# Fixing the order of GpSimd and of the transfer queue in a fused MoE, attention and recurrence kernel

## The chip, the core and the metric

The kernel runs on one core of one Trainium2 chip. The metric is the device time of one execution in microseconds (us). It has five instruction queues: PE (TensorE, matmuls; its weight loads are listed as PEld), ACT (ScalarE), DVE (VectorE), POOL (GpSimd) and SP (SyncE, which here does nothing but issue transfers). Each queue runs its own instructions in the order in which they stand in it, and waits at an instruction until what that needs is there.

## The reference, cut to what matters

The input is 2 sequences of 2048 tokens, 256 numbers each, all in float32. There are four parts, each adding to x:

```python
x = x + 0.5 * _L0_ffn_ref(_layernorm(x))   # 6 experts, top 2 of them per token, plus a shared expert
x = x + _L0_attn_ref(_layernorm(x))        # 16 heads of 16, every query sees all 2048 keys
x = x + 0.5 * _L0_ffn_ref(_layernorm(x))
x = x + 0.5 * _L1_ffn_ref(_layernorm(x))   # two steps of a gated recurrence, 6 + 6 + 2 products
x = x + _L1_attn_ref(_layernorm(x))        # causal, rotated queries and keys, clipped relative positions
x = x + 0.5 * _L1_ffn_ref(_layernorm(x))
```

In the second attention the relative position is clipped at 32, so it is the band of 32 keys before each query that gets its own term from `rel_emb`; the rest is one constant per query.

## The kernel before

**Stages.** The kernel is one Python trace, fully unrolled: `run_moe`, `attention0`, `run_moe`, `recurrence`, `attention1`, `recurrence`. x stays in SBUF. Blocks are of 512 tokens (`TB`), eight of them; scores and sums go through eight PSUM banks of 128 x 512.

**Mixture of experts (`moe`, from L166).** The tokens are treated in two halves. Each half is routed (`route`, `sort`), its normalised rows are scattered by GpSimd's indirect transfers into `places` in DRAM in the order of experts (`scatter`, L307), read back in 37 tiles of 128 rows (`experts`, L350: `tile_in`, `up`, `turn`, `down`), written to `results`, and gathered again with a weight (`combine`, L416, gathers at L423). The first half's gathers run beside the second half's tiles; half of the second half's gathers (`rest`) run inside the recurrence that follows.

**`attention0` (L661).** The work is cut in units: two per step, eight steps per group of 4 heads x 512 queries. In one unit PE does four score products for the largest (`largest`, L715, read by DVE at L719), four for the exponentials (`exponential`, L727, read by ACT at L732) and one sum over keys (`weighted`, L739). The sum is copied from PSUM by ACT (L605) and added to the group's running sum by POOL (L610, `gather`). Everything else (projections, layer norms, divisions) is put in lists of jobs by step. Keys and queries are spread to 32-row slots by small transfers on SP (`spread`, L134); rows of padding come from DRAM too (`pad_keys`, L141).

**`attention1` (L904).** The same in units of its own planner: `Ms`, `Me` are a group's first and last step of largest scores, `Es`, `Ee` of exponentials, `Rs` the step of the sum over relative positions. One group's band goes a long way: `by_position` (L1019) makes the products with `relk`, ACT sends them to DRAM (L1026, on ACT's own queue), `band_load` (L1036, SP, 1280 KB) reads them back skewed, DVE adds them to the scores (L1083), POOL subtracts the maximum (L1097), `band_store` (L1105, SP, 1280 KB) writes them out, `positions_load` (L1182, SP) reads them along the diagonal. Queries and keys are rotated (`rotate`, L959 to L976): ACT copies the projection, DVE exchanges neighbours (L969), POOL does two products and a sum (L971 to L975). When each transfer is emitted is a list `sends` of its own, in units.

**What sets the order.** The whole trace is in `tc.manual_schedule(engines=ENGINES)` with

```python
ENGINES = {mybir.EngineType.PE, mybir.EngineType.Activation, mybir.EngineType.DVE}
```

An engine in that set issues its instructions in the order of the trace. POOL and SP are not in it: a scheduler places their instructions by its own model of when each is ready. Inside `moe`, and inside the first `recurrence`, a second region orders POOL; but these are two regions, and where an instruction of one falls among those of the other is the scheduler's.

Of the kernel before, what the change touches and what calls it, by code (L numbers as in the profile page):

```python
# [17 lines left out]
P = 128  # L18
# [24 lines left out]
def macaron_kernel(ctx: ExitStack, tc: tile.TileContext, t: dict, out: bass.AP):  # L43
# [112 lines left out]
    ENGINES = {mybir.EngineType.PE, mybir.EngineType.Activation, mybir.EngineType.DVE}  # L156
# [9 lines left out]
    def moe(w, ws, gate_w, gate_b, rev, tri, iota, z, behind, last, gathered):  # L166
# [3 lines left out]
        with ExitStack() as s:  # L170
# [179 lines left out]
            def experts(h, exi, between):  # L350

                xT, h_, hT, val = {}, {}, {}, {}
                GROUP = 8

                def tile_in(i):
                    if i % GROUP == 0:
                        n = min(GROUP, NST - i)
                        _, vs = nc.values_load_multi_w_load_instructions(
                            exi[0:1, i : i + n], engines=[mybir.EngineType.PE],
                            min_val=0, max_val=(NE - 1) * EW,  # L360
                            skip_runtime_bounds_check_because="a sum of five comparisons times EW",
                        )
                        for k, v_ in enumerate(vs):
                            val[i + k] = v_
                    xs = wk.tile([P, D], F32, name="xs", bufs=4)
                    nc.sync.dma_start(out=xs, in_=places[h][ts(i, P), :])
                    pt = bank()
                    for kc in range(2):
                        nc.tensor.transpose(pt[:, ts(kc, P)], xs[:, ts(kc, P)], ident)
                    xT[i] = wk.tile([P, D], F32, name="xT")  # L370
                    nc.scalar.copy(xT[i], pt[:, 0:D])  # L371

                def up(i):
                    pu = bank()
                    for kc in range(2):
                        nc.tensor.matmul(  # L376
                            pu, lhsT=xT[i][:, ts(kc, P)], rhs=w[:, kc, ds(val[i], 2 * D)],
                            start=kc == 0, stop=kc == 1,
                        )
                    sg = wk.tile([P, D], F32, name="sg")  # L380
                    nc.scalar.activation(sg, pu[:, 0:D], AF.Silu)  # L381
                    h_[i] = wk.tile([P, D], F32, name="h")
                    nc.vector.tensor_tensor(h_[i], sg, pu[:, D:], ALU.mult)  # L383

                def turn(i):
                    ph = bank()
                    for kc in range(2):
                        nc.tensor.transpose(ph[:, ts(kc, P)], h_[i][:, ts(kc, P)], ident)
                    hT[i] = wk.tile([P, D], F32, name="hT")
                    nc.vector.tensor_copy(hT[i], ph[:, 0:D])  # L390

                def down(i):
                    po = bank()
                    for kc in range(2):
                        nc.tensor.matmul(  # L395
                            po[:, 0:D], lhsT=hT[i][:, ts(kc, P)],
                            rhs=w[:, kc, ds(val[i] + 2 * D, D)],
# [5 lines left out]

                tile_in(0)
                for i in range(NST + 2):
                    between(i)
                    if i + 1 < NST:
                        tile_in(i + 1)
                    if i < NST:
                        up(i)  # L410
                    if 0 <= i - 1 < NST:
                        turn(i - 1)
                    if 0 <= i - 2 < NST:
                        down(i - 2)
# [17 lines left out]
            def first_half(i):  # L432
                if 3 <= i < 3 + HC:
                    combine(0, i - 3)
# [5 lines left out]
            with tc.manual_schedule(engines={mybir.EngineType.Pool}):  # L440
                stats(0)
                stats(1)
                norm(0)
                stats(2)
                norm(1)
                shared_part(0, 0)
                shared_part(0, 1)
                stats(3)
                norm(2)
                shared_part(0, 2)  # L450
                norm(3)
                shared_part(0, 3)
                mul(0)
                stats(4)
                route(0)
                up(1)
                e0 = sort(0)
                stats(5)
                down(0)
                scatter(0)  # L460
                mul(1)
                up(2)
                stats(6)
                up(3)
                mul(2)
                norm(4)
                norm(5)
                stats(7)
                scatter(1)
                scatter(2)  # L470
                scatter(3)
                down(1)
                mul(3)
                down(2)
                norm(6)
                norm(7)
                down(3)
                route(1)
                up(4)
                mul(4)  # L480
                e1 = sort(1)
                down(4)
                up(5)
                mul(5)
                for b in range(HB, NTB):
                    scatter(b)
                down(5)
                experts(0, e0, lambda i: None)
                experts(1, e1, first_half)
                up(6)  # L490
                mul(6)
                chunks = iter(range(HC))

                def rest(n):
                    for _ in range(n):
                        c = next(chunks, None)
                        if c is not None:
                            combine(1, c)
                            last(c)

                rest(2)
                up(7)
                mul(7)
                rest(1)
                down(6)
                rest(1)
                down(7)
                rest(4)
                if gathered is None:
                    rest(HC)  # L510
# [12 lines left out]

    class Pieces:
# [3 lines left out]
        def __init__(self, s, name, norm, weights_o, bias, queries):  # L528
            self.keep = pool(s, name + "_keep")
            self.wk = pool(s, name + "_wk", 2)  # L530
            self.norm, self.wo, self.bias = norm, weights_o, bias
            self.mnegs = []
# [8 lines left out]
            self.cn, self.cT, self.o, self.pTs, self.q = ({} for _ in range(5))  # L541

# [26 lines left out]
        def values(self, v, wv, b, qc, half, row):  # L569

            w = HV * VW
            nc.gpsimd.memset(v[:, :, w:], 0.0)
            dst = v[:, :, 0:w].rearrange("p k (h d) -> p k h d", d=VW)
            nc.gpsimd.memset(dst[:, :, :, DH:], 1.0)
# [10 lines left out]
            else:  # L585
# [4 lines left out]
                )  # L590

# [10 lines left out]
        def gather(self, t, pv, parts, q0=0):  # L602
# [7 lines left out]
            nc.gpsimd.tensor_tensor(o, o, part[:, q0:], ALU.add)  # L610
# [39 lines left out]
    class Jobs(dict):  # L650
        def at(self, step, fn, *args):
            self.setdefault(step, []).append((fn, args))

        def run(self, step):
            for fn, args in self.get(step, ()):
                fn(*args)


    def attention0(norm, tail, wq, wk_, wv, wo, bff):
# [7 lines left out]
        with ExitStack() as s:  # L667
# [25 lines left out]

            def vals(b, half, qc):
                if qc == 0:
                    v[b, half] = vpool.tile([P, NKB, HV * VW + DH - 1], F32, name="v", bufs=3)
# [78 lines left out]

            for step, fn, *args in tail:
                at(PER * NG + step, fn, *args)
            for step in range(min(jobs), max(jobs) + 1):
                todo = jobs.get(step, [])
                for n in range(2):  # L780
                    te, tm = (step - 9) // PER, step // PER
# [11 lines left out]
                    if 0 <= unit < NG * NKB:  # L793
                        weighted(unit // NKB, unit % NKB)

# [135 lines left out]
    def attention1(norm, tail, w, relk, relv, kbias, dramp, skew):  # L931
# [4 lines left out]
        with ExitStack() as s:  # L936
# [24 lines left out]
            def rotate(wa, b, qc, g, bias):  # L961
# [9 lines left out]
                e.tensor_tensor(xa, xa, cos[b, qc], ALU.mult)  # L971
                e.tensor_tensor(xb, xb, sin[b, qc], ALU.mult)
                if bias is not None:
# [549 lines left out]
```

## Time and profile before

| | us |
|---|---|
| median of 3 runs (4281.06 to 4286.72) | 4283.15 |
| profiled execution | 4171.17 |
| its span | 4169.4 |
| PE busy in the span | 4036.9 |
| SP waiting at L1036 (`band_load`), 22 waits | 285.4 |
| SP waiting at L134 for POOL L975 (a rotation), 27 waits | 257.3 |
| SP waiting at L1105 (`band_store`) for POOL L1097, 21 waits | 244.4 |
| POOL waiting at L610 for ACT L605, 610 waits | 1401.6 |

The profiled execution was 112 us shorter than the median. PE is busy for most of the span, but busy time says little alone: the granted clock has to be read beside it, and so has the stage. The stages, by what PE does, are: first mixture 0 to 350, first attention 350 to 2100, second mixture 2100 to 2445, first recurrence 2445 to 2622, second attention 2622 to 3950, last recurrence to the end.

### The profile page before, as it was taken

The numbers are of one execution on the slowest core, as the hardware profiler recorded it, in microseconds if no ns is written. First come the engines' busy times: TensorE is split into PE (matmuls) and PEld (weight loads), VectorE is DVE, ScalarE is ACT, GpSimd is POOL, SyncE is SP. The second block draws the span as 40 slices with busy tenths as digits, with TensorE's granted clock in tenths as the row PEclk, the third lists the DMA queues.
The fourth block names the chain that finished last, engine by engine and source line by source line (L and its number), as shares of the span: only waits on it lengthen the run. The fifth ranks groups of instructions, "written<-read, shape, count | busy, mean of one in ns | idle before, by whom it ended". The sixth has DMA issues, their size and how long they took to land.

```text
span 4169.4 us, 78015 instructions
## 1 busy us (share of the span) xinstructions
PE 4036.9 (97%) x28256; PEld 1967.4 (47%) x28256; DVE 2697.1 (65%) x6122; ACT 2498.5 (60%) x5091; POOL 1692.5 (41%) x1606
## 2 busy tenths in 40 slices
PE   8997999999999999999999989899999999999999
PEld 4665533333333333333356645555554455555445
DVE  6242888888877788888752444666577666667533
ACT  2331488888877888888933322355557666556832
POOL 4254133336433333333442430445545654544510
PEclk9998899999999999999999999999999999999999
DMA  7343000000000000000043410445433344452101
GB/s 254 119 125 86 15 4 4 4 4 4 4 14 14 4 4 4 4 4 5 9 171 118 127 60 5 106 98 114 95 86 67 81 95 92 86 106 53 45 22 41
DMA packets 376879, 245.34 MB, mean 59 GB/s; under 512 B 157232, under 2 KB 349104, under 8 KB 376496
## 3 DMA queue, kind: packets, MB, share of 16 engines
q1 hardware_dynamic: 298160, 198.39, 18.6%
q0 software_dynamic: 12288, 33.57, 2.5%
q10 hardware_dynamic: 66048, 8.39, 1.4%
q8 instruction: 226, 3.70, 0.4%
q14 instruction: 157, 1.29, 0.1%
HBM read 118.36 MB, written 105.12 MB: 54 GB/s over the span
## 4 chain that ended last, share of the span: by engine, by line
PE 84%; POOL 5%; DVE 4%; DMA 3%; issue 2%; SPq 2%; ACT 1%; ACTq 0%; POOLq 0%; DVEq 0%
PE s L727 13%; PE s L739 12%; PE s L715 10%; PE s L146 8%; PE s L376 6%; PE s L1173 6%; PE s L1059 6%; PE s L1144 5%; PE s L395 3%; DMA band<-skew 2%; PE s L642 1%; POOL places L311 1%; PE s L1154 1%; PE s L1158 1%; PE s L1137 1%
## 5 line engine op out<-in xcount | busy, mean ns | idle before, releaser
L610 POOL TENSOR_TENSOR part<-part 128x512 f32<-128x512 f32 (+3 forms) x800 | 962.6, 1203 | 1407.2 <-ACT part L605 1401.6
L719 DVE TENSOR_REDUCE mx<-s 128x1 f32<-128x512 f32 x2048 | 1270.1, 683 | 331.2 <-PE s L715 331.2
L732 ACT ACTIVATE pT<-s 128x512 f32<-128x512 f32 x2048 | 1063.4, 618 | 239.2 <-PE s L715 237.9
L715 PE MATMUL s<-kT,q 32*128 32x512 f32 x4096 | 1031.9, 630 | 0.0
L727 PE MATMUL s<-q,kT 32*128 32x512 f32 x4096 | 1013.6, 615 | 0.0
L1165 ACT ACTIVATE pT<-s 128x512 f32<-128x512 f32 (+3 forms) x1280 | 588.8, 542 | 223.8 <-PE s L1144 122.3
L605 ACT COPY part<-s 128x512 f32<-128x512 f32 (+3 forms) x864 | 506.5, 587 | 287.9 <-PE s L1173 149.7
L727 PEld LDWEIGHTS s<-q,kT 32*128 32x128 f32 x4096 | 417.9, 184 | 467.2 <-DVE mx L719 326.9
L1067 DVE TENSOR_REDUCE mx<-s 128x1 f32<-128x512 f32 (+1 forms) x768 | 473.3, 679 | 179.5 <-PE s L1059 171.9
L739 PE MATMUL s<-pT,v 128*32 128x512 f32 x4096 | 549.9, 605 | 0.4
L715 PEld LDWEIGHTS s<-kT,q 32*128 32x128 f32 x4096 | 426.4, 187 | 125.5 <-ACT pT L732 77.8
L1059 PE MATMUL s<-kT,q 32*128 32x512 f32 (+7 forms) x2240 | 329.6, 433 | 3.6 <-ACT part L605 3.6
L1173 PE MATMUL s<-pT,v 128*32 128x512 f32 (+3 forms) x2560 | 307.9, 549 | 13.1 <-DVE mx L1083 12.8
L376 PE MATMUL s<-we,xT 128*128 x592 | 279.0, 594 | 0.6 <-ACT xT L371 0.6
L1083 DVE CUSTOM_DVE_ANT_0 band<-s,band 128x160 f32<-128x160 f32 (+1 forms) x512 | 156.1, 316 | 173.2 <-PE s L1059 98.9
L1059 PE MATMUL s<-b,q 32*128 32x512 f32 (+7 forms) x1280 | 246.6, 527 | 13.1 <-ACT part L605 8.6
L383 DVE TENSOR_TENSOR h<-sg,s 128x256 f32<-128x256 f32 x148 | 62.4, 421 | 296.3 <-ACT sg L381 296.3
L739 PEld LDWEIGHTS s<-pT,v 128*32 128x32 f32 x4096 | 82.4, 108 | 335.7 <-ACT pT L732 297.4
L1144 PE MATMUL s<-q,kT 32*128 32x512 f32 (+3 forms) x1152 | 235.5, 509 | 0.0
L423 POOL DMA_INDIRECT yg<-results,at x128 | 125.1, 977 | 232.3 <-DMA results<-y 83.1
L1144 PE MATMUL s<-q,b 32*128 32x512 f32 (+3 forms) x896 | 213.8, 583 | 0.0
L1097 POOL TENSOR_TENSOR band<-band,mneg 128x640 f32<-128x640 f32 x128 | 161.1, 1261 | 97.2 <-DVE mneg L1093 91.4
(207 smaller groups left out, 5159.7 us busy)
## 6 DMA issues: line engine op xcount, KB each, us to landing
band<-skew SPq DMA_DIRECT2D x32, 1280.0 KB
pd<-band SPq DMA_DIRECT2D x32, 1280.0 KB
xs<-places SPq DMA_DIRECT2D x148, 128.0 KB
results<-y SPq DMA_DIRECT2D x148, 128.0 KB
places<-zero SPq DMA_DIRECT2D x2, 4736.0 KB
we<-in_we SPq DMA_DIRECT2D x12, 768.0 KB
skew<-s ACTq DMA_DIRECT2D x32, 256.0 KB
s<-pd SPq DMA_DIRECT2D x32, 256.0 KB
```

Source lines behind the costliest of these rows:

```text
L376: nc.tensor.matmul(pu, lhsT=xT[i][:, ts(kc, P)], rhs=w[:, kc, ds(val[i], 2 * D)], start=kc == 0, stop=kc == 1,)
L605: nc.scalar.copy(part[:, q0:], pv[:, q0:])
L610: nc.gpsimd.tensor_tensor(o, o, part[:, q0:], ALU.add)
L715: nc.tensor.matmul(ps, lhsT=q[t][rows(j), ts(qb, P)], rhs=kT[b, g][rows(j), ts(kc, TB)], start=True, stop=True,)
L719: nc.vector.tensor_reduce(mx[t][:, qb * J + j, kc : kc + 1], ps, AX.X, ALU.max)
L727: nc.tensor.matmul(st, lhsT=kT[b, g][rows(j), ts(kb, P)], rhs=q[t][rows(j), :], start=True, stop=True,)
L732: nc.scalar.activation(z.pTs[t, kb, j], st, AF.Exp)
L739: nc.tensor.matmul(pv[rows(j), :], lhsT=v[b, g // 2][:, kb, ds(h * VW, 32)], rhs=z.pTs.pop((t, kb, j)), start=True, stop=True,)
L1059: nc.tensor.matmul(ps[:, ds(cols, n)], lhsT=lhsT, rhs=kT[b, c, g][rows(j), ds(k0, n)], start=True, stop=True,)
L1144: nc.tensor.matmul(ps[:, q0:], lhsT=k, rhs=q[t][rows(j), q0:], start=True, stop=True, skip_group_check=True,)
L1165: nc.scalar.activation(z.pTs[t, kb, j][:, q0:], st.pop((t, kb, j))[:, q0:], AF.Exp)
L1173: nc.tensor.matmul(pv[rows(j), q0:], lhsT=v[b, kb // CPB, g // 2][:, kb % CPB, ds(h * VW, 32)], rhs=z.pTs.pop((t, kb, j))[:, q0:], start=T ...
```

## The change

**All five queues in the order of the trace.** `ENGINES` takes in POOL and SP, and the inner regions go.

**Work moved a unit later.** `Pieces` gets a list of work that is due later. `begin` is called at the start of each unit, and runs what is due in it. The causal and other partial sums (L610), the subtraction on the band (L1097) and the rotations on POOL (L971 to L975) are emitted through it, one unit after their place of before.

```diff
+        def later(self, units, fn, *args):
+            self.due.at(self.unit + units, fn, *args)
+        def begin(self, unit):
+            self.unit = unit
+            self.due.run(unit)
+            self.due.pop(unit, None)
...
-            nc.gpsimd.tensor_tensor(o, o, part[:, q0:], ALU.add)
+            self.later(1, nc.gpsimd.tensor_tensor, o, o, part[:, q0:], ALU.add)
...
-                nc.gpsimd.tensor_tensor(
-                    band[t][:, qb], band[t][:, qb],
+                z.later(
+                    1, nc.gpsimd.tensor_tensor, band[t][:, qb], band[t][:, qb],
...
+                if step < 0:
+                    turn()
+                else:
+                    z.later(1, turn)
```

(`turn` is the rotation's three or four instructions as before.) The first band memset of a group at the start of a sequence, L1080, goes from POOL to DVE.

**Due units of the transfers in `attention1`.** With `Rs` one step later:

```diff
-                Rs.append(start + 4)
+                Rs.append(start + 5)
...
-                sends.at(2 * early[n] + (2 if early[n] < 0 else 3), queries_out, n)
+                sends.at(2 * early[n] + (2 if early[n] < 0 else 5), queries_out, n)
...
-                            due = 2 * (f - 6 + (qc == 0)) + (2 if f < 6 else 3)
+                            due = 2 * (f - 6 + (qc == 0)) + (2 if f < 6 else 5)
...
-                sends.at(2 * by + 2, band_load, n)
-                sends.at(2 * Me[n] + 3, band_store, n)
-                sends.at(2 * Rs[n] - 6, positions_load, n)
-                sends.at(2 * Rs[n] - 3, positions_exp, n)
+                sends.at(2 * by + 3, band_load, n)
+                sends.at(2 * Me[n] + 4, band_store, n)
+                sends.at(2 * Es[n] + 3, positions_load, n)
+                sends.at(2 * Es[n] + 6, positions_exp, n)
```

**Values' padding.** The columns of ones and zeros in the value tiles were set by two POOL memsets (L572, L574) for every block of values. The tiles are now taken once (3 in `attention0`; 8 in `attention1`, from the pool `keep` instead of `wk`) and padded once each, by two ACT instructions (`pad_values`: a copy with scale 0, and one with scale 0 and bias 1).

**One loop over the experts' tiles.** `experts` runs over the 74 tiles of both halves in one pipeline. A tile's read from DRAM (`fetch`) is emitted three tiles ahead of its use, and was emitted one tile ahead. The first half's gathers start four tiles into the second half, and started three into it.

```diff
+                for n in range(3):
+                    fetch(n)
                 tile_in(0)
+                for n in range(N + 2):
+                    if n >= NST:
+                        between(n - NST)
+                    if n + 3 < N:
+                        fetch(n + 3)
+                    if n + 1 < N:
+                        tile_in(n + 1)
...
```

**Order of the loads in `run_moe`.** The shared expert's weights `ws` are the second load, and were the sixth; the zeros of the first half's `places` go before the experts' weights and those of the second half behind them; the next stage's weights are loaded by a function called after both (before, those of the recurrence stood ahead of the second `run_moe`). `fill_skew`, 32 transfers of 144 KB into `skew`, moves from behind `attention0` to step 60 inside it.

## The prediction

> **What bounds the kernel now.** I read the page first, then the stretches by stage, then the waits of PE, then the order of instructions around each long wait. The page says that PE is the bound:
>
> ```profile
> PE 4036.9 (97%) x28256; PEld 1967.4 (47%) x28256; DVE 2697.1 (65%) x6122; ACT 2498.5 (60%) x5091; POOL 1692.5 (41%) x1606
> PEclk9998899999999999999999999999999999999999
> ```
>
> So 132 us of the span are without PE work, and the granted clock falls in places. Stretches by stage (length, busy time and count of PE, PEld, DVE, ACT, POOL; then clock, transfer share, GB/s) tell where:
>
> ```profile
> 350.00:455.00 105.00, 78.81 (x300) 58.32 (x298) 50.22 (x89) 10.58 (x18) 19.52 (x43) 0.70 0.27 72
> 455.00:2100.00 1645.00, 1638.47 (x12856) 613.49 (x12856) 1308.71 (x2203) 1347.11 (x2619) 660.81 (x554) 1.00 0.02 6
> 2445.00:2500.00 55.00, 40.11 (x99) 18.65 (x99) 25.26 (x67) 15.77 (x25) 18.34 (x21) 0.84 0.13 38
> 2622.00:2700.00 78.00, 63.76 (x441) 40.12 (x439) 54.81 (x164) 23.22 (x45) 36.82 (x52) 0.89 0.55 130
> 2700.00:3950.00 1250.00, 1215.62 (x10868) 643.83 (x10864) 823.02 (x2450) 786.80 (x1682) 647.47 (x603) 0.98 0.40 86
> ```
>
> The body of the first attention has nothing to give (99.6% busy at full clock). What can be won lies at the seams and in the second attention: 34 us there without PE, and 28.5 us of clock (sum of 1 minus clock over its slices of 50 us). Both follow from single waits:
>
> ```profile
> PE s L119 <- DVE b L109: 15.5, 7, 12.0
> PE s L1173 <- DVE mx L1083: 12.8, 4, 4.1
> PE s L1059 <- ACT part L605: 12.2, 7, 3.1
> ```
>
> (us in total, times, longest.) The timeline shows what stands behind each. The 12 us wait (POOL's lines on either side of it):
>
> ```profile
> 2443.23 0.95 POOL L423 DMA_INDIRECT yg<-results,at  x1 [0.30 <-issue]
> ...
> 2453.24 0.95 POOL L423 DMA_INDIRECT yg<-results,at  x1 [0.30 <-issue]
> 2454.23 0.25 POOL L96 TENSOR_SCALAR ve<-mv 128x4 f32<-128x4 f32 x1
> ```
>
> DVE's statistics (L92) for this norm were done at 2447.4, but POOL had nine gathers of the recurrence's region ahead of L96. L98 followed at 2455.71 and PE's transposes at 2457.36. The 4 us waits: a band's load (SP, L1036) issued just behind another band's store (L1105):
>
> ```profile
> 2867.38 0.38 SPq L1105 DMA_DIRECT2D pd<-band  x1
> 2867.88 1.20 SPq L1036 DMA_DIRECT2D band<-skew  x1
> ```
>
> The chain of waits gives this load 14.04 us, and gives the one of 2653.82, with no store before it, 6.62. DVE (L1083) waits for it, and PE for the banks that DVE holds. The 3 us waits: ACT issues its transfer to `skew` only when one that SP has just issued has landed, and everything of ACT stands behind it:
>
> ```profile
> 2722.03 0.40 ACTq L1026 DMA_DIRECT2D skew<-s  x1
> 2722.52 0.59 ACT L605 COPY part<-s 128x512 f32<-128x512 f32 x1 [4.70 <-DMA q<-s]
> ```
>
> SP had issued those q at 2719.39, seven units ahead of their first use.
>
> **What the Trainium skill says.** *PSUM — Partial Sum Buffer*, section "Engine vs sequencer instructions": the queues of ScalarE, VectorE and GpSimd are strictly first in, first out. The trace agrees: L96 ran after the gathers before it, 7 us after its input. *DMA: Bandwidth & Descriptors*, section "Queues, rings and completion order": each of the 16 DMA engines takes a queue's descriptors in ring order. The 14.04 against 6.62 us fit: store and load together take twice one of them. *TensorE: Matmul & The Clock Gate*, section "What's actually happening": the clock is halved unless PE was busy lately, and comes back after some microseconds of work. Here: clock 0.50 from 2450 to 2460, 0.64 to 2465, then 1.00; so an idle stretch costs more than itself.
>
> **The change part by part.** The sum is made against the profiled execution, 4171.2 us (span 4169.4).
>
> *A. `ws` second in the queue.* PE waits 2.86 us at 15.09 for `ws` (landing 5.4 us after its issue at 12.40), which stood behind five small loads. Issued some 3 us earlier, it lands before PE asks. Next in line are the norms of the blocks of x that follow, on DVE. -2.5 (-2.9 to 0).
>
> *B. Start of the first attention (350 to 417).* SP bounds it: eight keys, each 8 pads (3.8 us) and 8 spreads (4.9 us), 8.9 us per key in the timeline, with ACT's copies (`packed`, 2 buffers) behind. Before, SP began with 17 pads at 349.90, while the queries were projected. In trace order the 8 spreads of queries come first, and can start when ACT's copy of 351.62 is done, at 352.2: +2.3 us. Sixteen padding instructions on ACT before L584 cost, by the nearest row (ACT, 128x96, 283 ns), 4.5 us; PE's wait is at the key copies before them and DVE paces what follows, so they are hidden but for a bank or two. +3 (+2 to +7).
>
> *C. `fill_skew` at step 60.* 32 transfers, 17.2 us of SP by the row at 2099.17. Steps are 5.9 us here, so SP is busy until 3 steps later, and the queries of step 62 are issued some 2 us late for a use at step 64, 11.7 us after their projection; the spread takes 5 us and lands in 2. Just hidden. In the second mixture it lay in front of the experts' weights, which PE did not wait for: no gain. Eight more paddings on ACT, 83% busy, may show: +2 (0 to +5).
>
> *D. Second mixture to recurrence.* In trace order L96 stands behind the eight gathers of its own part only (until about 2443.2), waits for 2447.4, then 0.25 + 1.04 on POOL, DVE's first L109 at 2448.9, PE at 2449.5: 7.9 us of 12 go. Of the clock loss in this stretch, 0.16 x 55 = 8.8 us, some 4 go. Behind the waiting L96 are the sixteen gathers of the recurrence, now from 2449 to 2470 (1.25 each) against 2443 to 2469; the next norm that needs them had its L96 at 2478.9, and would have it at 2471: just free. -11 (-13 to -6).
>
> *E. Recurrence to second attention (2622 to 2660).* Two effects. Before, 16 pads were issued at 2585 and 4 at 2628; now the pads of each key stand behind the spreads before them: 16 x 0.48 = 7.7 us of SP come between the queries' spreads (2635.1) and the first rows that PE needs (L1059 at 2650.4). But the tables (`cos`, `sin`) waited for the recurrence's last sums (2626.9), whose memory they shared; with 19 KB of value tiles put before them they need not share it, and DVE's first product (2633.6) can start at 2627.6. If so: queries 2629.8 to 2634.8, pads, keys, pads, first rows at 2651.9, +1.5, and the band 1.3 us earlier. If not, +8. I take +1 (-2 to +8).
>
> *F. Second attention.* Three edits, one effect: the transfers' order. With `band_load` at 2By+3 and `band_store` at 2Me+4, and SP in that order, the load of the group (0,0,1), unit 57, precedes the store of its neighbour, unit 58; it issues at about 2867 and lands in 6.6 us, at 2874, before PE stalled (2878.3). The four waits of this kind go: 12.8 us. The queries' spreads, now 5 units after their projection, stand behind a `band_load` which itself needs ACT's L1026; so L1026 no longer finds a fresh spread before it. Five waits (2720, 2942, 2984, 3295, 3642) of 2.78 + 2.68 + 1.41 + 3.12 + 1.40 = 11.4 us go. The nine gaps carry the 28.5 us of clock; I count two thirds as time, 19. Together 43. What is behind the waits now: on SP, spreads behind a `band_load` that waits for L1026 to land (3.85 us at 2642.40), which the planner's 9 units (28 us) from a query's spread to its scores cover; on POOL, sums behind a rotation (5.3 us) or a norm (6.2), one unit of 3.2 us later than now, with 5 buffers for `part`, of which three are held where the short groups overlap. I take a quarter off for that: -32 (-43 to +40).
>
> Moved at nothing: the sums of the first attention (same order among themselves, hidden by PE's 24 matmuls of a unit, 2.93 us against 1.26; uncovered, one add), the single loop (PE idles 0.4 us between the halves; a tile takes 3.02 us, so a read two tiles ahead has 6 us for its 2.9), 64 memsets of POOL (9.5 us, idle there).
>
> Sum: -2.5 + 3 + 2 - 11 + 1 - 32 = -39.5, so 4171.2 becomes 4131.7. The median stood 112 us above that execution, for a reason that the profile does not show; I take the difference over: 4283.15 - 39.5 = 4243.6.
>
> **The rivals.** *The waits of the second attention are replaced, not removed* (chance 0.2): each transfer in order waits for one of ACT, POOL and SP, so another of the kind comes up; A to E stand, F gives nothing to -10: about 4271. For it: SP already waits 285 us at L1036. Against: no such wait is near PE's first use.
>
> *More than counted* (0.1): F in full and the tables free, -43 - 11 - 2.5 + 3 = about -54, and the band's chain shortens the steps after each gap: about 4222.
>
> *Slower* (0.15): POOL in strict order. A rotation or a norm waiting at POOL's head holds the sums, `part` runs out of its 5 buffers, ACT stops at L605, PE has no banks. Price of each: 2.6 us and 3.2 of clock (28.5 / 9), 5.8. 29 rotations run on POOL (L971 x29); with eighteen such stalls among them, and F's 43 still won, +104 - 43 - 8 = +53: 4336. It decides from nine stalls on, where 9 x 5.8 = 52 takes up those 51. Against: POOL is 52% busy there, and the sums now come a unit after ACT's copy.
>
> **Chances.** Forecast (gain of 20 to 50) 0.55, replaced 0.2, more 0.1, slower 0.15. 0.2% of 4283 is 8.6 us, about what can be told from no change. Replaced gives faster in two of three cases: faster 0.55 + 0.1 + 0.13 = 0.78, same 0.08 (its rest, and one in ten of slower), slower 0.14. The range: 43 + 13 + 3 + some clock on one side gives 4200; on the other all upper bounds of B, C and E with F at nothing come to about +7: 4290.
>
> **What would show it.** A: no PE wait for `ws`. B: PE's L715 first at 419 to 423. D: one L96 and L98 within 2 us of the statistics, and the L119 wait at most 4 us. E: the first L1059 of the second attention 28 to 30 us after the recurrence's last product. F: no load of 14 us in the chain, the row "L1173 <- L1083" gone, L1026 right behind L1024, clock above 0.99 there. Wrong if ACT's idle time at L605 grows with POOL named at L610's side, or if SP's waits at L1036 come with waits of PE for q or kT.

## The result and the profile after

The changed kernel takes 4305.86 us (median of 5 runs, 4300.59 to 4309.12), the kernel before in the same comparison 4283.36 us (5 runs, 4281.06 to 4287.99): ratio 1.0048, 95% interval 1.0033 to 1.0062. It is slower by 0.5%; the forecast was 4243.6, faster.

The page of the changed kernel, with PE's busy time and, in 40 slices, its granted clock:

```profile
PE 4070.4 (95%) x28256; PEld 1979.7 (46%) x28256; DVE 2702.6 (63%) x6130; ACT 2509.4 (58%) x5131; POOL 1686.3 (39%) x1534
PEclk9899599999999999999998999999999999999999
```

This profiled execution (span 4304.0) stands where the timed ones do; the one of the kernel before, 4171.2, did not. So the kernel before was profiled again, unchanged, as the first run below (`e1_before_again`): 4283.83 us, span 4282.1.

```profile
PE 4068.2 (95%) x28256; PEld 1978.6 (46%) x28256; DVE 2695.0 (63%) x6122; ACT 2499.8 (58%) x5091; POOL 1694.7 (40%) x1606
PEclk9899699999999999999998999999999999999999
```

That is the one to compare with. The timelines give the first or last product of PE in each stage; the table has the stretches between these products, in us ("predicted" is the step's term of the sum; `in_c` is the recurrence's first product, `uo` the first of its outputs):

| stretch | before again | changed | difference | predicted |
|---|---|---|---|---|
| start to the last expert tile | 378.2 | 379.0 | +0.8 | A -2.5 |
| the same to the first largest product | 95.5 | 114.6 | +19.1 | B +3 |
| on to the router of the second mixture | 1696.8 | 1700.0 | +3.2 | C +2 |
| on to the product with `in_c` | 372.8 | 374.1 | +1.3 | 0 |
| recurrence, to its first product with `uo` | 102.2 | 97.7 | -4.5 | D -11 |
| rest of it | 94.9 | 94.9 | 0 | 0 |
| its last product to the first largest product | 22.8 | 27.7 | +4.9 | E +1 |
| second attention, to its last weighted product | 1318.8 | 1315.4 | -3.4 | F -32 |
| rest | 200.1 | 200.6 | +0.5 | 0 |
| sum | 4282.1 | 4304.0 | +21.9 | -39.5 |

Three terms carry the miss: F (29 us), B (16) and D (6.5). What took the place of the waits is in the waits of PE (us in total, times, longest). Changed kernel:

```profile
PE s L609 <- ACT packed L743: 50.5, 7, 18.4
PE s L663 <- POOL part L541: 31.2, 9, 7.3
...
PE s L1132 <- DMA b<-s: 10.2, 1, 10.2
```

Kernel before, profiled again (L578, L619 and L1059 are the lines that became L609, L663 and L1132):

```profile
PE s L578 <- ACT packed L690: 23.5, 5, 6.4
...
PE s L1173 <- DVE mx L1083: 14.9, 4, 4.3
...
PE s L1059 <- ACT part L605: 12.0, 7, 2.9
PE s L619 <- POOL part L610: 8.6, 5, 2.2
```

F's two rows (L1173 behind DVE, L1059 behind ACT's copies) are gone, as predicted. In their place PE waits for POOL's sums (L541 is now the line that issues whatever was put off): 31.2 us against 8.6 over the whole kernel.

**Where B's time went.** POOL in the changed kernel (start, duration; in brackets the idle time before and its end) at the start of the first attention:

```profile
424.13 0.95 POOL L436 DMA_INDIRECT yg<-results,at  x1 [0.30 <-issue]
425.38 0.95 POOL L436 DMA_INDIRECT yg<-results,at  x1 [0.30 <-issue]
426.33 1.00 POOL L555 MEMSET mneg<- 128x512 f32 x2
427.25 1.00 POOL L580 MEMSET q<- 128x512 f32 x2
```

and ACT beside it:

```profile
401.96 0.60 ACT L763 ACTIVATE packed<-s 128x512 f32<-128x512 f32 x1 [12.06 <-PE s L146]
403.07 0.58 ACT L743 COPY packed<-s 128x512 f32<-128x512 f32 x1 [0.52 <-PE s L146]
434.63 0.58 ACT L743 COPY packed<-s 128x512 f32<-128x512 f32 x1 [30.97 <-DMA q<-packed]
```

The queries were ready to be spread at 402.6, when ACT's copy ended. Their tiles had yet to be cleared by POOL, and this 1.0 us of clearing stood behind the gathers of the second half (and the clearing of `mneg`) until 427.3. SP's spreads began at 427.82; ACT waited 31 us for its buffer, PE for ACT. The scheduler of the kernel before had put the clearing of `q` ahead of those gathers (first profile):

```profile
316.88 1.93 POOL L547 MEMSET q<- 128x512 f32 x4
```

It was done 33 us before ACT's copy of the queries ended, at 352.2.

**Where F's time went.** DVE's and POOL's part in one of the two waits of 7.3 us; the first fence is DVE, the second POOL:

```profile
3115.64 0.01 DVE L1029 LOAD_MASK_SELECT s<-s  x1 [5.37 <-PE s L1274]
3115.64 0.75 DVE L1029 STREAM_SHUFFLE s<-s 128x512 f32<-128x512 f32 x1
```

```profile
3116.47 1.27 POOL L1033 TENSOR_TENSOR s<-s,cos 128x512 f32<-128x512 f32 x1 [4.87 <-DVE s L1029]
3117.69 1.28 POOL L1034 TENSOR_TENSOR s<-s,sin 128x512 f32<-128x512 f32 x1
3119.07 1.57 POOL L1036 TENSOR_SCALAR s<-s,rel_col 128x512 f32<-128x512 f32 x1
3120.72 1.26 POOL L1037 TENSOR_TENSOR s<-s,s 128x512 f32<-128x512 f32 x1
3121.94 1.26 POOL L541 TENSOR_TENSOR part<-part 128x512 f32<-128x512 f32 x1
3123.16 1.26 POOL L541 TENSOR_TENSOR band<-band,mneg 128x640 f32<-128x640 f32 x1
3124.38 2.49 POOL L541 TENSOR_TENSOR part<-part 128x512 f32<-128x512 f32 x2
```

The exchange of neighbours (L1029) writes a tile named `s2`. That name has four buffers, shared by the rotated tiles, the products by position and the position tiles. DVE waited 5.4 us for PE's product with `relv` (L1274), the last reader of a position tile; the rotation stood at POOL's head, and behind it another sum, a band's subtraction and, done at 3125.65, the last sum of a group, for which PE waited from 3118.37 to 3125.69 in front of divide's transposes. The change moves the product with `relv` one step later (`Rs` +4 to +5) and holds rotated tiles two units longer.

### The profile page after: what moved, and what is told of

It is laid out like the page before. It is cut to its first block, busy times and chain, and to the rows that moved or that the text cites. A ratio compares the mean times of both kernels' runs of the same rounds, so it can differ in the third digit from the quotient of the medians.

```text
span 4304.0 us, 77994 instructions
## 1 busy us (share of the span) xinstructions
PE 4070.4 (95%) x28256; PEld 1979.7 (46%) x28256; DVE 2702.6 (63%) x6130; ACT 2509.4 (58%) x5131; POOL 1686.3 (39%) x1534
## 4 chain that ended last, share of the span: by engine, by line
PE 83%; DVE 4%; issue 4%; POOL 3%; SPq 2%; another core or an unknown queue 1%; ACT 1%; DMA 1%; POOLq 0%; DVEq 0%; ACTq 0%
PE s L784 13%; PE s L796 12%; PE s L772 10%; PE s L146 9%; PE s L1246 6%; PE s L1132 6%; PE s L383 5%; PE s L1217 5%; PE s L403 3%; PE s L686 1%; PE s L1227 1%; PE s L1231 1%; PE s L1210 1%; PE s L344 1%
## 5 line engine op out<-in xcount | busy, mean ns | idle before, releaser
L541 POOL TENSOR_TENSOR part<-part 128x512 f32<-128x512 f32 (+3 forms) x800 | 961.7, 1203 | 1457.8 <-ACT part L649 1452.8
L1132 PE MATMUL s<-kT,q 32*128 32x512 f32 (+7 forms) x2240 | 330.7, 435 | 0.6 <-ACT part L649 0.6
L383 PE MATMUL s<-we,xT 128*128 x592 | 289.4, 612 | 13.5 <-issue 12.5
L1132 PE MATMUL s<-b,q 32*128 32x512 f32 (+7 forms) x1280 | 248.5, 522 | 10.3 <-DMA b<-s 10.2
L541 POOL TENSOR_TENSOR band<-band,mneg 128x640 f32<-128x640 f32 x128 | 161.3, 1260 | 137.8 <-DVE mneg L1166 94.2
```

The source lines that it names most:

```text
L383: nc.tensor.matmul(pu, lhsT=xT[n][:, ts(kc, P)], rhs=w[:, kc, ds(val[n], 2 * D)], start=kc == 0, stop=kc == 1,)
L1132: nc.tensor.matmul(ps[:, ds(cols, n)], lhsT=lhsT, rhs=kT[b, c, g][rows(j), ds(k0, n)], start=True, stop=True,)
```

## The experiments

Each ratio is to the kernel before on the same chip; that kernel took 4287.66 us (22 runs) beside e1 to e4, 4290.96 (36) beside e5 to e8, 4171.57 (20) beside e9 to e11 and 4172.79 (7) beside e12, so ratios and stretches are compared, not times across chips.

**e1_before_again**: no edit.

> The kernel before, unchanged, to profile it once more. Theory: its ordinary executions (4283) hold stalls of PE in the two mixtures like those of the changed kernel (85 us of gaps without a wait that the profile names, and a lower clock), and the profiled execution of 4171 lacked them; then this profile spans about 4280, with PE some 110 us less busy or slower before 420 and between 2210 and 2480 us, and the rest as in the first profile within 5 us. Rival: the change brought the mixtures' stalls; then this profile shows no gaps there, and if it spans 4280 the 112 us sit elsewhere.

4283.83 us. Up to the first largest product it is 58.1 us behind the first profile (473.7 against 415.6), from there to `in_c` of the recurrence 54.4 more, and after that within 0.3 us of it all the way (1738.7 against 1738.6). The 112 us of the first comparison lie in the mixtures and what follows the first; the change did not bring them.

**e2_first_q_on_act** (`first_on_act` is true in `attention0` alone; `...` stands for the rest of an operand)

```diff
-                nc.gpsimd.memset(self.q[t + i], 0.0)
+                if t or not self.first_on_act:
+                    nc.gpsimd.memset(self.q[t + i], 0.0)
+                else:
+                    nc.scalar.activation(self.q[t + i]..., ident..., AF.Copy, scale=0.0)
```

> The changed kernel with the first two query tiles of the first attention cleared by ACT, so that this clearing no longer stands behind POOL's 32 gathers. Theory: the clearing behind the gathers holds SP's spreads of queries for 25 us, so the time falls by 22 to 28 us, to 4278 to 4284, and the first largest product comes about 66 us after the projection of its queries instead of 94. Rival: the 64 pads and spreads of keys on SP bound the start anyway; then less than 8 us is won, 4298 or more.

Ratio 1.0004 (0.9995 to 1.0012): 0.44% less than the changed kernel, 19 us, a little under the forecast. Projection of the queries to first largest product: 78.2 us, from 94.2 (75.1 in the kernel before, profiled again). SP's spreads began as soon as ACT's copy was there:

```profile
400.88 5.24 SPq L134 DMA_DIRECT2D q<-packed  x8
```

**e3_sp_free and e4_pool_free**: SP, or POOL, out of `ENGINES`.

```diff
-    ENGINES = {E_.PE, E_.Activation, E_.DVE, E_.Pool, E_.SP}
+    ENGINES = {E_.PE, E_.Activation, E_.DVE, E_.Pool}        # e3
+    ENGINES = {E_.PE, E_.Activation, E_.DVE, E_.SP}          # e4, POOL in order inside moe alone
```

> The changed kernel with the transfer queue's order left to the scheduler again, POOL still in program order. Theory: program order on SP costs about 5 us at the start of the second attention (pads behind spreads) and takes away some 20 us of waits at band loads; without it those waits come back (row of PE's scores waiting for DVE at mx, four times 3 to 4 us), 4310 to 4325. Rival: SP's order makes the stalls of the mixtures (loads of expert tiles behind stores of results); then these stalls go and the time is 4220 or less.

> The changed kernel with POOL left to the scheduler as in the kernel before (in order within a mixture alone), SP in program order. Theory: POOL's order costs about 25 us at the start of the first attention and 20 to 30 us of waits of PE for the last sum of a group in the second attention, and wins 9 us between mixture and recurrence: 4255 to 4275. Rival: the sums put one unit later make those waits, whatever the order: 4285 to 4292, with the row PE (transposes of divide) waiting for POOL's sums still at 25 us or more.

e3: 1.0045 (1.0029 to 1.0062), no difference in the total, but parts that cancel: the first attention starts 9.1 us sooner (85.1 from its projection), the second 6.6 (11.2 from `relk` to the first largest product, 17.8 with SP in order), and the second lasts 10.0 longer (1325.4), half of what the theory had; the rest, 4 us, is in the first mixture. e4: 0.9975 (0.9966 to 0.9984), so POOL's order costs 31 us, of it 14.5 at the start of the first attention and 15.0 in the second (1300.4); at the recurrence it gains 3.3. The waits for sums halve, to 15.9 us, and don't vanish. DVE waits for the product with `relv` as before, but neither of PE's 7.3 us waits is left (the longest is 3.5): it is POOL's strict order that hands a held buffer on to PE.

```profile
DVE s L1030 <- PE s L1275: 10.7, 2, 5.4
```

**e5_position_step_back and e6_sums_at_once** take the two explanations of the waits for sums apart.

```diff
-                Rs.append(start + 5)
+                Rs.append(start + 4)                          # e5
-                end = max(Rs[n], Ee[n] + 1)
+                end = max(Rs[n] + 1, Ee[n] + 1)               # e5
-            self.later(1, nc.gpsimd.tensor_tensor, o, o, part[:, q0:], ALU.add)
+            nc.gpsimd.tensor_tensor(o, o, part[:, q0:], ALU.add)   # e6, in attention1
```

> The changed kernel with the transposes and products by position of the second attention one step earlier, as before (Rs at +4), divide where the change has it. Theory: the change holds the four buffers of s2 longer (a rotated tile two units, a position tile one step), DVE's shuffle waits at its head for a buffer (5.4 us for the product with relv), POOL's rotation behind it and the last sum behind that: then the two PE waits of 7.3 us (at divide's transposes) go with their clock loss, 15 to 20 us: 4285 to 4291. Rival: the sums are late by their unit of delay alone, and the shuffle would wait for the next holder of s2 (the spread): less than 6 us, 4299 or more, both waits of over 4 us still there.

> The changed kernel with the sums of the second attention issued at once again and not a unit later (rotations and band sums still later, POOL and SP in order). Theory: on a POOL in strict order the sum a unit later stands behind the next rotation, and the last sum of a group is late for divide; at once, PE's waits for POOL's sums (31.2 us, 9 times) fall under 10 us, and 20 to 28 us with the clock are won: 4278 to 4286. Rival: the sum waits as long behind the rotation of its own unit, and DVE's shuffle (s2) is what holds POOL: under 8 us, 4298 or more.

e5: 0.9980 (0.9972 to 0.9989), 0.68% under the changed kernel, 29 us, more than the theory's 15 to 20. e6: 1.0047 (1.0031 to 1.0062), nothing won, and PE still waits 27.1 us for sums: its rival holds. The waits of DVE for the shuffle tell why; the changed kernel, e6 (L1029 is L1032 there) and e5:

```profile
DVE s L1029 <- PE s L1274: 10.7, 2, 5.4
```

```profile
DVE s L1032 <- PE s L1277: 10.7, 2, 5.4
```

```profile
DVE s L1029 <- ACT s L1027: 25.3, 23, 2.0
DVE s L1029 <- DMA q<-s: 8.7, 1, 8.7
```

With the product a step earlier the row is gone, and PE's waits for sums are 8.1 us. The second attention lasts 1289.9 us, 25.5 less.

**e7_pads_first**

```diff
                     keep_k[qc, g] = z.keep.tile([P, TB], F32, name=f"kT{qc}{g}")
+                    if qc == 1:
+                        pad_keys(keep_k[qc, g])
...
-                    if qc == 0 or b == 0:
+                    if qc == 0 or b == 0 and qc > 1:
```

> The changed kernel with the 16 pads of the first keys of the second attention ahead of everything else of that stage on SP. Theory: eight of them stand between the spreads of queries and of keys and hold the first largest product by 4 us: it comes about 13.5 us after the first product with relk instead of 17.8, total 4300 to 4303. Rival: the memory of these keys is free only with the recurrence's end, so the pads now hold the tables and the queries instead: no gain or a loss up to 8 us.

Ratio 1.0031 (1.0019 to 1.0043); `relk` to the first largest product 13.7 us, 4.1 less. The stretch shows the gain; the total alone would not (its interval overlaps that of the changed kernel).

**e8_all_four**: e2, e5, e6 and e7 together.

> All four together: first queries cleared by ACT (measured: -16 to -18), position products a step earlier, sums of the second attention at once, pads first. Theory: the changed order then keeps what it won (waits at band loads, the norm behind gathers): 4306 - 17 - 25 (the two edits in the second attention overlap) - 4 = 4260 (4250 to 4270), faster than the kernel before by 0.4 to 0.9%. Rival: new waits of the same kind take their place in the second attention: 4280 or more.

Ratio 0.9989 (0.9982 to 0.9995), worse than e5 alone: the rival. The second attention lasts 1310.3 us, 20.4 more than in e5, and the sums at once are the only further edit inside it. DVE's copy of a position tile into `s2` waits longer for a rotation, 23.8 us where e5 has 12.6 in as many waits (waits of DVE), and one such place on POOL shows why:

```profile
DVE s L1284 <- POOL s L1049: 23.8, 5, 5.7
```

```profile
2971.41 1.27 POOL L662 TENSOR_TENSOR part<-part 128x512 f32<-128x512 f32 x1 [4.97 <-ACT part L656]
2972.64 1.26 POOL L541 TENSOR_TENSOR band<-band,mneg 128x640 f32<-128x640 f32 x1
2973.86 1.28 POOL L1045 TENSOR_TENSOR s<-s,cos 128x512 f32<-128x512 f32 x1
```

The sum stands at POOL's head for 5.0 us until ACT has copied it, and the rotation, whose input DVE had ready by 2969.3, behind it. A unit later the copy is there. So the delay of the sums is a gain, once `s2` is free in time (e9 below, without the sums at once, has 1284.0 us).

**e9_three_and_pads**: e2, e5 and e7, and the pads of part 0 with their own spread.

```diff
             def keys_out(b, qc, g, i):
+                if qc == 0:
+                    pad_keys(kT[b, qc, g + i])
                 spread(kT[b, qc, g + i], packed[b, qc, g], i)
```

> First queries cleared by ACT, position products a step earlier (sums of the second attention still a unit later), the 16 pads of the second attention first, and the pads of its keys of part 0 issued with their own spreads and no longer ahead of the queries' spreads. Theory: the sums at once were what took back 20 us in the kernel with all four (DVE's copy of a position tile waiting for POOL's rotation 23.8 us); without them the ratios add: 0.998 of the kernel before, less 16 at the start of the first attention, 4 at that of the second and 6 for the wait behind eight pads: about 0.992 (4256 where before has 4290), second attention from its first largest product on about 1284. Rival: what is won at the start is lost further on: 0.996 or more.

Ratio 0.9904 (0.9888 to 0.9921): 4133.91 us where the kernel before has 4171.57. It beats both kernels. The edit of the pads is aimed at one wait of the changed kernel, where SP had eight pads in front of a spread, and DVE's shuffle needed the buffer that this spread reads (SP, then DVE):

```profile
3429.64 7.70 SPq L141 DMA_DIRECT2D b<-in_pads  x8
3437.43 5.63 SPq L134 DMA_DIRECT2D q<-s  x8
```

```profile
3444.76 0.01 DVE L1029 LOAD_MASK_SELECT s<-s  x1 [8.24 <-DMA q<-s]
```

PE stood still for 5.29 us at 3440.92. The longest gap of PE in that stage of e9 is 2.4 us.

**e10_divide_too**: as e5, with divide moved as well (`end` as in the changed kernel).

> Position products and divide both a step earlier (all of Rs back at +4), the rest as changed. Theory (buffers of s2): DVE's two waits of 5.4 us for the product with relv stay away, since the position tile is free a step earlier; PE waits for the last sums only as long as the sum is late by its unit, 2 to 4 us each, none of 7: 4285 to 4296 where the kernel with divide unmoved had 4282. Rival (slack of divide alone): with the distance from product to divide as in the changed kernel, both waits of 7.3 us are back and the time is that of the changed kernel, 4300 or more.

Ratio 0.9974 (0.9964 to 0.9985), the gain of e5 again. No shuffle waits for the product with `relv`, and PE waits for sums 9.4 us in 5 waits of at most 2.2. It is the buffer, not the distance from product to divide.

**e11_back_sp_free**: e5 with SP out of `ENGINES`.

> The kernel with position products a step earlier, and the transfer queue left to the scheduler. Theory: SP's order is what removes the waits at band loads and behind fresh spreads (predicted 24 us and their clock); without it some of them return, in the second attention 10 to 25 us more than the 1289.9 of the kernel with SP in order, less 6 at its start: 4286 to 4302. Rival: the later sums and rotations removed them, not SP's order: second attention within 4 us of 1290, total 4275 to 4280.

Ratio 1.0009 (1.0000 to 1.0018), 0.35% over e10 (14 us). The second attention lasts 1313.4 us, and both waits of the kernel before are back, the first nearly in full, the second in part:

```profile
PE s L1246 <- DVE mx L1156: 11.0, 3, 4.8
PE s L663 <- POOL part L541: 8.1, 4, 2.2
PE s L1132 <- ACT part L649: 7.1, 5, 3.6
```

So SP's order does what F said. In this stage it is worth 23.5 us against e5 (1289.9, with SP's order the only difference, but on another chip) and 30.5 against e10 (1282.9, on the same chip, with divide moved too), less 7 at its start and 8 at that of the first attention.

**e12_before_step_later**: the kernel before with the later step alone.

```diff
-                Rs.append(start + 4)
+                Rs.append(start + 5)
-                sends.at(2 * Rs[n] - 6, positions_load, n)
-                sends.at(2 * Rs[n] - 3, positions_exp, n)
+                sends.at(2 * Rs[n] - 8, positions_load, n)
+                sends.at(2 * Rs[n] - 5, positions_exp, n)
```

> The kernel before with one part of the change alone: transposes and products by position (and divide, which follows them) one step later, their loads and exponentials where they were. Theory: the position tile holds its buffer of s2 a step longer, DVE's shuffle waits for the product with relv at two or more places (about 5 us each) and PE behind it, whatever the order of POOL: slower by 8 to 25 us, ratio 1.002 to 1.006, with a row of DVE (stream shuffle) waiting for the product with relv. Rival: the wait needs the rotation a unit later and POOL in order as well; then no such row and a ratio of 0.999 to 1.001.

Ratio 1.0096 (1.0080 to 1.0113), 41 us. The step costs without any other part, and more than either theory had: PE's waits for POOL's sums grow from 9.4 us to

```profile
PE s L619 <- POOL part L610: 39.0, 13, 5.2
```

The row that the theory named is not there. Two shuffles do wait 5.2 and 5.4 us, and the profile puts that to a copy of ACT; but the waits that DVE works through just before are for the eight transfers that spread the queries rotated before, and they go on when the last of these lands, at 3134.0 and at 3809.8. The first of the two places:

```profile
3130.67 1.25 SPq L134 DMA_DIRECT2D q<-s  x1
3134.33 0.01 DVE L969 LOAD_MASK_SELECT s<-s  x1 [5.21 <-ACT part L605]
```

So here too a buffer of `s2` is held, by a rotated tile until it is spread and not by a position tile; PE waits 4.2 us for a sum behind each of the two. What makes the rest of the 39.0 us was not followed.

The stretch of the second attention in the kernel before (first profile), changed, e5, e9 and e12 (length, PE busy and count, the other engines, clock, transfer share, GB/s), the same 11344 matmuls each time:

```profile
2650.40:3969.30 1318.90, 1279.91 (x11344) 675.04 (x11344) 865.61 (x2588) 823.51 (x1754) 689.77 (x638) 0.97 0.41 87
```

```profile
2788.00:4103.40 1315.40, 1274.76 (x11344) 671.62 (x11344) 863.65 (x2596) 830.16 (x1766) 689.30 (x616) 0.98 0.40 88
```

```profile
2795.20:4085.10 1289.90, 1265.88 (x11344) 664.94 (x11344) 865.03 (x2596) 829.49 (x1766) 690.06 (x616) 0.99 0.42 89
```

```profile
2646.50:3930.50 1284.00, 1261.80 (x11344) 662.43 (x11344) 864.75 (x2596) 829.41 (x1766) 690.71 (x616) 0.99 0.42 90
```

```profile
2651.70:4013.50 1361.80, 1297.59 (x11344) 682.02 (x11344) 863.92 (x2588) 825.25 (x1754) 690.46 (x638) 0.97 0.41 85
```

Length minus busy is PE's idle time: 39.0, 40.6, 24.0, 22.2 and 64.2 us. The changed kernel has no less of it than the one before: the waits were exchanged, not removed.

## Why the prediction was wrong, step by step

**F is the step that failed most**: "Three edits, one effect: the transfers' order." There was a fourth edit in the diff, `Rs` one step later, which the prediction did not price and did not mention, and a side of the later rotations and spreads that it did not see: they hold `s2` (no run takes this side alone). The mechanism was right (e11: without SP's order both rows return; e5 and e10: with the step back the stage is 28.9 and 36.0 us shorter than before, against -32). In the changed kernel the held buffer ate nearly all of it: the stage came out at -3.4, and e5, which frees the buffer, is 25.5 us below that. It took POOL's strict order as well: with POOL free (e4) and the buffer held, 15.0 of them come back. What was listed as behind the waits ("sums behind a rotation") was the right pair of instructions. The price was missing because the rotation's own wait was not followed to its cause, the buffer that its input is written to. The rival "replaced" named the outcome of this stage; "slower" named its path, with `part` as the buffer that runs out, and it was `s2`.

**B failed by an omission.** +3 counted SP's and ACT's instructions. It said of the queries' spreads that they "can start when ACT's copy of 351.62 is done", and did not ask which queue clears their destination. POOL in program order clears it behind 32 gathers: 16 us on one chip (e2), 22 on another (90.9 in e10, 68.7 in e9). With that taken away the stretch is 68.7 against 65.9 us (e9 and the first profile) or 78.2 against 75.1 (e2 and e1): +2.8 or +3.1, the predicted +3. The passage of the Trainium skill, *PSUM — Partial Sum Buffer*, "Engine vs sequencer instructions" (queues first in, first out), which the prediction cites for D where it helps, was the reason here too; the trace agrees, 25 us from queries ready to tiles cleared.

**D was counted twice in part.** The wait went from 12.0 to 2.5 us, 9.5 where 7.9 were worked out (a later one of the same kind grew by 1.2), but of the clock some 4 us were added as though they were lost beside the wait. The stretch of the kernel before (first profile) and of e10, from `in_c` to the first product with `uo`, and the wait itself in the kernel before:

```profile
2430.80:2533.00 102.20, 86.96 (x242) 41.74 (x241) 46.24 (x119) 26.78 (x42) 31.45 (x36) 0.92 0.11 31
```

```profile
2457.10:2554.80 97.70, 90.21 (x242) 42.36 (x241) 46.52 (x119) 27.10 (x42) 31.61 (x36) 0.93 0.11 33
```

```profile
2445.40:2457.40 12.00, 0.04 (x1) 0.07 (x1) 2.47 (x10) 0.00 (x0) 9.44 (x12) 0.69 0.33 99
```

0.31 x 12.0 = 3.7 us of the clock loss lay inside the wait, where PE had nothing to slow down. In e10 the same 242 matmuls are busy 3.3 us longer: clock is still lost, now while PE works. Idle time falls by 7.8 us, the stretch by 4.5. Of the 3.3 us, 1.7 lie in a dip to half clock for 3.4 us from 2461.2 on, before which PE is listed as busy without a gap, near the end with 24 products of one column (`in_c`). The first profile and e9 have no dip there; why it comes was not tried.

**E** was +1 within -2 to +8 and came out at +4.9. Its case "if so" held, the tables were there in time, but this gave 1.3 us and not the 5.3 of the sum (queries' spreads at 2629.8 for 2635.1). In the first profile DVE stands idle for 0.9 and 0.4 us before its first two products with the tables (at 2632.52 and 2633.62), in the changed kernel not at all; but DVE comes to them only when the recurrence's last sums are done, at 2631.0 in the first profile. The rest is SP's pads between the spreads; e7 takes 4.1 away.

**A failed in its mechanism.** `ws` was issued 3.1 us sooner (9.10, from 12.21 in the kernel before, profiled again), but it did not land before PE asked. PE's wait for it there, and in the changed kernel:

```profile
PE s L146 <- DMA ws<-in_ws: 2.6, 1, 2.6
```

```profile
PE s L146 <- DMA ws<-in_ws: 2.3, 1, 2.3
```

PE's first product with `ws` moved from 17.72 to 17.32: the transfer, issued sooner, took 8.2 us until then in place of 5.5. So the four small loads that it passed had held it by hardly more than 0.4 us; what else held it stays open. The table's +0.8 can't tell: in e2 to e8 the same stretch takes 377.0 to 383.1 us. In e10 and e11 that mixture ends 1.7 and 3.2 us sooner than in the first profile, which looks like A's -2.5, but PE waits 2.3 and 2.2 us for `ws` there too. That is luck.

**C and the rest** hold in size: C +2 (+3.2; between +0.2 and +4.2 in the ten later kernels with it, though no run takes C's edits alone), the single loop within 1.3 us.

**The base was sound** for the other terms: the 112 us that the prediction carried over are the same in e1, 103.6 of them in the mixtures and 9.2 in B's stretch. Without the held buffer and the late clearing the sum would have come out near: e9, which has both mended, is 38.4 us below the first profile in its spans, 4131.0 against 4169.4, by stages -2.2 (A), +2.8 (B), +2.5 (C), -0.2, -5.5 (D), -1.2 (E), -35.0 (F) and +0.5. That it comes so near -39.5 is luck in part: D is 5.5 short, A's place is filled by something else, and e9 moves pads that the prediction left where they were, in E and before the wait of 5.3 us in F.

## What to carry to other kernels

When a queue goes into program order, price not the instructions that are seen to move but those that used to be hoisted: every clearing, pad or load whose result is needed early now stands behind all that was issued before it. And when a step is moved later, list the buffers that it holds until then and who next asks for one: a ring of four under one name that three engines share carries a stall from PE to DVE, from DVE to POOL and back. An idle stretch and its low clock are one loss where they overlap; add only the part of the clock that falls on work.

## What the runs showed of the hardware

The same kernel took 4283 to 4291 us in three comparisons and 4172 to 4173 in two; the four whose chip is on record ran on four chips (the first profile, 4171, is like the latter two). All of the difference is made in the mixtures and at the start of what follows the first. While POOL issues its indirect scatters, the kernel before, profiled again, shows waits of up to 10.8 us on PE, ACT and DVE that end with nothing the profile names (up to 14.0 in the changed kernel). One window in the kernel before, profiled again, and ACT at the router:

```profile
130.00:140.00 10.00, 3.04 (x6) 0.62 (x5) 0.84 (x2) 0.38 (x1) 7.57 (x9) 0.67 0.26 105
```

```profile
82.18 0.59 ACT L207 COPY lgT<-s 128x512 f32<-128x512 f32 x1 [10.78 <-remote]
```

In the first profile the window from 130 to 140 has PE busy throughout at full clock, and this copy starts 0.1 us after the router's product as modelled (76.27, product to 76.17); here it starts 6.1 us after it (product to 76.03). From 160 us on, with the scatters issued, PE has no wait over 2.1 us in this mixture. The packets of the scatters took the same time in both (mean 118 ns, and 119 in the first profile, in the stretch from 60 us to the first expert product), so longer packets don't explain it. The cause was not tried and stays open.
